# A four-layer convolution net on one core: start-up transfers on one queue, and M's first piece eight steps later

## The chip, the core and the metric

The kernel runs on one core of a Trainium2 chip. The core has five engines with instruction streams of their own: TensorE (matmul, PE in the profile), VectorE (DVE), ScalarE (ACT), GpSimd (POOL) and SyncE (SP, which here only issues transfers). A transfer is issued by an instruction of one of the engines and then moved by the core's DMA engines. The metric is the device time of one execution in microseconds (us), the median of several.

## The reference

The input is x, four images of 32 x 32 points with 16 channels. Four layers each add to x a function of its group norm. Three of them are position-dependent convolutions, the third in order is an interval layer:

```python
def conv(inputs, M, W, G):                    # layers 0, 1 and 3
    first = einsum('ijyx,byxc->bijc', M, inputs)
    shifted = conv_with_kernel(inputs, G)      # a 3x3x16x16 kernel for each of the 1024 points ij
    diff = relu(inputs[:, None, None] - shifted)
    second = einsum('ijyx,bijyxc->bijc', W, diff)
    return first - second

x = x + conv(gn(x), L0_M, L0_W, L0_G)
x = x + conv(gn(x), L1_M, L1_W, L1_G)
x = x + interval_layer(gn(x), W0, b0, W1, b1, W2, b2)
x = x + conv(gn(x), L3_M, L3_W, L3_G)
```

For each point ij, each of 16 output channels and each image, `shifted` is a whole 32 x 32 image, from a product over 9 x 16 = 144 inputs. That product is nearly all of the work. The term with M is one matrix product of 1024 x 1024 with the images.

## The kernel before

**Tiling.** The images are handled in two groups (g = 0, 1) of two images (b = 0, 1). A convolution layer of one group is a *phase*; with three convolution layers there are six. A phase runs over eight chunks t of 128 points each, and in a chunk over 16 channels f and two images b, so 32 *steps*. `conv_layer` writes out the steps. A step makes one 128 x 1024 product in a pair of PSUM banks: `first_part` (matmuls of `ib` and `ia` with the G's parts, then at L665 a scaling of the PSUM pair on ScalarE) and, one step later, `second_part` (matmuls of `iyz` and `im`, then at L682 on VectorE the minimum with zero, times W, summed). There are four PSUM pairs. In the steady state a step takes TensorE 1.57 us.

**Preparing G.** Four channels of a chunk are a *unit* u of 8 steps. `prep_parts` prepares each unit before it is used, a piece at each step: `raw` is loaded from HBM (L110), GpSimd subtracts a selection (L214, in `prep`), VectorE masks the upper bits (L203, `upper`), ScalarE makes W9 (L175, `halve`) and two of the parts (L236, L240), GpSimd the rest (L237, L238, L241, L243, L245). Last, two copies within SBUF, issued by SyncE, turn the halves of the partitions (L251, `parts<-parts`), and the `raw` of the unit after next is loaded. The first two units are taken as plain fp32 without this preparation, so the first 16 steps of the kernel run on other tiles (`raw`, `first`) and take 1.94 us each.

**Preparing the images.** For each image, `split` makes two parts (`ty` on ScalarE at L284, `tz` on VectorE or GpSimd at L280) in a tile `temp`. `place` then copies them to the partitions of `ia` (eight copies, L299) and `ib` (four copies, L302), and `difference` makes `iyz` (L288). In the first phase this is done by `rest_of_start` within the first steps, on VectorE, with `temp` a piece of the tile `first`; in later phases by `before_conv`, on GpSimd. `place` there is given a list of engines and issues its copies on them in turn: `[nc.sync, nc.scalar]` at the start (so ScalarE issues all copies of `tz`), `[nc.sync]` later.

**The term with M.** `load_first_terms` takes the tile `mt` and loads M in eight pieces of 512 KB, one every six steps (L416). `first_terms` then runs 128 matmuls (L427), two transposes (L434) and two additions to X (L437). `first`, `temp`, `mt` and the tables of the interval layer all have the same single buffer (`tag="big"`), so the first piece of M waits until the copies out of `temp` have read it.

**Order.** The schedule is the program's own: each engine runs its instructions in the order in which they are written. `behind(phase)` is a generator of the side work of a phase. `conv_layer` advances it after a step; the number that it yields is how many steps pass until it is advanced again, and the constants `IDLE` and `CALM` wait for a step at which the preparation of G leaves room. An instruction that waits holds up everything behind it on its engine, and this holds for an engine that issues a transfer too. The transfers of SyncE and ScalarE get one of eight semaphores in turn, in the order of the program, and each waits before its issue until the transfer that had the semaphore before has landed. An example: the eighth copy of an image, issued at 259.35 us, came directly after the landing at 259.33 us of the G that had been issued eight transfers earlier.

The constants `wv` and `bv` of the interval layer (L449, L450) and X of the second group (L739) are loaded by ScalarE.

Of the kernel before, what the change touches and what calls it, by code (L numbers as in the profile page):

```python
# [29 lines left out]
LAST = (H - 1) * HW  # L30
# [14 lines left out]
def net_kernel(ctx: ExitStack, tc: tile.TileContext, x, xq, xi, convs, iv_w, iv_b, out):  # L45
# [26 lines left out]
    nc = tc.nc  # L72
# [20 lines left out]
    X = [const.tile([P, NT, GC], F32, name=f"X{g}") for g in range(NG)]  # L93
# [80 lines left out]
    def halve(dst, src, mask):  # L174
        nc.scalar.activation(dst, src, AF.Copy, scale=mask[:, 1:2])  # L175
# [20 lines left out]
    def image(v, x):  # L196
        return v.rearrange("... (y x) -> ... y x", x=x)[..., :HW]
# [69 lines left out]
    def prep_plain_rest(u, at=0, to=FU):  # L267
        halve_rest(units[u][3][:, at:to], raws[u][:, 2, at:to], low_p)

    def halves(temp, b):  # L270
        v = temp.rearrange("p (k s b n) -> p k s b n", k=2, s=2, b=GB)
        return v[:, 0, :, b], v[:, 1, :, b]

    def split(eng, g, b, temp, name, pause=IDLE):

        ty, tz = halves(temp, b)
        high = upper(image(raw[:, :2, b], WP), 2, f"x{name}{b}")
        yield 1
        for s in range(2):
            eng.tensor_tensor(  # L280
                image(tz[:, s], HW), image(raw[:, s, b], WP), image(high[:, s], HW), ALU.subtract
            )
            yield pause
            nc.scalar.activation(ty[:, s], high[:, s], AF.Copy, scale=EPS)  # L284
# [2 lines left out]
        ty, tz = (v.bitcast(F32)[:, s] for v in halves(temp, b))  # L287
        eng.tensor_tensor(iyz[g][:, s, b], ty, tz, ALU.subtract)  # L288

    def place(engs, g, b, temp):  # L290

        ty, tz = (v.bitcast(F32) for v in halves(temp, b))
        da, db = (v[g].bitcast(F32)[:, :, b] for v in (ia, ib))
        k = 0
        for h, (lo, hi) in enumerate(QUARTERS):
            for s in range(2):
                at = HW if s == h else 0
                for to, src in ((lo, ty), (hi, tz)):
                    engs[k % len(engs)].dma_start(da[to, s, :LAST], src[lo, s, at : at + LAST])  # L299
                    k += 1  # L300
            for to, src in ((lo, ty), (hi, tz)):
                engs[k % len(engs)].dma_start(db[to], src[hi])  # L302
                k += 1
        yield 1


# [64 lines left out]
    def before_conv(g, layer):  # L371
        xn = work.tile([P, NT, GC], F32, tag="xn", bufs=2, name=f"xn_{g}_{layer}")
        xns[g] = xn
        yield from group_norm(g, f"c{g}{layer}", xn, 1 if layer == 2 else 4)

        nc.vector.transpose(
            xt[g][:, :, 1 : 1 + H], xn
        )  # L380
        inner = xs[g][:, :, WP : WP + H * WP].rearrange("p h (t r n) -> p h r t n", r=ROWS, n=WP)
        for r in range(ROWS):
            for h in range(2):
                nc.sync.dma_start(
                    inner[:, h, r], xt[g][GC * r : GC * (r + 1), :, HW * h : HW * h + WP]
                )
        yield 2
        xsv = xs[g].rearrange("(b c) h n -> c h b n", b=GB)
        for slot, row, tap in [
            (slot, row, tap) for slot in range(2) for row, tap in enumerate(TAPS[slot])  # L390
        ] + [(2, row, 8) for row in range(4)]:
            for h in range(2):
                off = tap // 3 * WP + tap % 3
                r0 = 64 * h + C * row
                nc.sync.dma_start(
                    raw[r0 : r0 + C, slot ^ h if slot < 2 else 2, :, :RUN], xsv[:, h, :, off : off + RUN]
                )
            if layer < 2 or row % 2:
                yield 1
        yield 6 if layer == 2 else 12  # L400
        temp = big.tile([P, 8192], F32R, tag="big", name=f"temp_{g}{layer}")[:, :TEMP]
        for b in range(GB):
            yield from split(nc.gpsimd, g, b, temp, f"{g}{layer}")
            yield IDLE
            halve(image(im9[g][:, b], HW), image(raw[:, 2, b], WP), low_x)
            yield from place([nc.sync], g, b, temp)
            for s in range(2):
                difference(nc.gpsimd, g, b, s, temp)
            yield 1
            halve_rest(image(im9[g][:, b], HW), image(raw[:, 2, b], WP), low_x)  # L410
            yield 1

    def load_first_terms(layer):
        mt = big.tile([P, NT, 4, 256], F32, tag="big", name=f"MT_{layer}")
        for pt in range(NT):
            nc.sync.dma_start(mt[:, pt], convs[layer][0][pt // (NT // 2)][:, pt % (NT // 2)])  # L416
            yield 6
        return mt
# [25 lines left out]
    wv = const.tile([P, 7, C], F32, name="wv")  # L444
    bv = const.tile([P, 3], F32, name="bv")
    iv = {}

    def constants():
        nc.scalar.dma_start(wv, iv_w)  # L449
        nc.scalar.dma_start(bv, iv_b)  # L450
        mask2 = const.tile([P, GB], F32, name="mask2")
        nc.vector.tensor_reduce(
            mask2, ident.rearrange("p (s b c) -> p b s c", b=GB, c=C), axis=AX.XY, op=ALU.add
        )

        nc.gpsimd.tensor_scalar_mul(mask2[GC : 2 * GC], mask2[GC : 2 * GC], -1.0)
        yield 2

        def blocks(dst, k, mask, n, p0=0):
            p = dst.shape[0]  # L460
            nc.gpsimd.tensor_tensor(
                dst,
                wv[p0 : p0 + p, k, :].unsqueeze(1).to_broadcast([p, n, C]),
                mask[p0 : p0 + p].unsqueeze(2).to_broadcast([p, n, C]),
                ALU.mult,
            )

        nc.gpsimd.memset(rt, 0.0)
        yield 1


        for k, hidden, name in ((0, None, "f0"), (3, 2, "f1"), (6, 5, "f2")):
            n = 64 if hidden is None else 96
            t = const.tile([n, GB, C], F32, name=name)
            blocks(t[:64], k, mask2, GB)
            if hidden is not None:
                blocks(t[64:], hidden, mask2, GB, 64)
            iv[name] = t.rearrange("p k c -> p (k c)")
            yield 1
        for k, name in ((1, "r0"), (4, "r1")):  # L480
            t = const.tile([64, NQ * GB, C], F32, name=name)
            for q in range(NQ):
                blocks(t[:, q * GB : (q + 1) * GB, :], k, mask2, GB)
            iv[name] = t.rearrange("p k c -> p (k c)")
            yield 1
# [249 lines left out]
    def behind(phase):  # L735
        g, layer = phases[phase]
        if phase == 0:
            yield from rest_of_start()
            nc.scalar.dma_start(X[1], x[1])  # L739
            zeros(1)  # L740
            yield 1
            yield from constants()
        if phase + 1 < len(phases):
            g1, layer1 = phases[phase + 1]
            if layer1 == 2:
                yield from interval_layer(g1)
            terms = g1 == NG - 1 and layer1 < NL - 1
            yield from before_conv(g1, layer1)
            if terms:
                mt = yield from load_first_terms(layer1)  # L750
                yield from first_terms(layer1, mt)
        if phase == len(phases) - 1:
            mt = yield from load_first_terms(layer)
            yield from first_terms(layer, mt)
            yield 4
            nc.sync.dma_start(out[1 - g], X[1 - g])
# [114 lines left out]
    def rest_of_start():  # L871

        nc.sync.dma_start(X[0], x[0])
        load_raw(2)
        load_raw(3)
        prep_plain_rest(0, F0, FU)
        for slot in (0, 1, 2):
            normal(nc.vector, 1, slot)
            sides(nc.vector, 1, slot)
        halve(image(im9[0][:, 1], HW), image(raw[:, 2, 1], WP), low_x)  # L880
        prep_plain(1)
        prep(2)
        yield 1
        halve_rest(image(im9[0][:, 1], HW), image(raw[:, 2, 1], WP), low_x)
        prep_plain_rest(1)
        yield 2
        temp = first.bitcast(F32R)[:, used : used + TEMP]
        for b in range(GB):
            yield from split(nc.vector, 0, b, temp, "00", 1)
            yield from place([nc.sync, nc.scalar], 0, b, temp)  # L890
            for s in range(2):
                difference(nc.vector, 0, b, s, temp)
            yield 1
        nc.gpsimd.memset(zero, 0.0)
        nc.vector.memset(part, 0.0)
        zeros(0)
        xns[0] = work.tile([P, NT, GC], F32, tag="xn", bufs=2, name="xn_00")
        yield from group_norm(0, "c00", xns[0], 4)
# [83 lines left out]
```

## Time and profile before

| | us |
|---|---|
| median of 3 runs | 2481.87 |
| lowest, highest | 2480.47, 2485.29 |
| the profiled execution | 2481.97 |
| its span, from the first to the last instruction | 2480.3 |

What each engine was busy with in five stretches of the span (the first numbers are start and end, then the length; x is the number of instructions; the last three are the granted clock of TensorE as a share, the mean share of busy DMA engines, and the GB/s that they moved):

```profile
core 0: us, PE busy (x) PEld busy (x) DVE busy (x) ACT busy (x) POOL busy (x), PEclk, DMA share, GB/s
0.00:46.00 46.00, 37.51 (x182) 18.79 (x182) 42.58 (x108) 11.72 (x20) 15.25 (x21) 1.00 0.73 215
46.00:56.00 10.00, 7.48 (x64) 5.94 (x66) 6.87 (x16) 6.89 (x9) 9.08 (x13) 1.00 0.32 74
56.00:248.00 192.00, 191.97 (x1716) 160.29 (x1714) 164.09 (x306) 150.62 (x178) 130.10 (x164) 1.00 0.57 156
248.00:276.00 28.00, 26.10 (x231) 21.21 (x229) 23.71 (x37) 19.87 (x23) 19.66 (x21) 1.00 0.76 196
276.00:447.00 171.00, 171.00 (x1593) 147.70 (x1591) 134.60 (x230) 126.03 (x144) 98.25 (x113) 1.00 0.55 153
```

The first phase runs from 0 to about 447 us. Between 56 and 248 us and from 276 us on, TensorE has no gap to speak of. The stretches 46 to 56 and 248 to 276 hold 2.5 and 1.9 us in which it ran no matmul.

How to read the lines below: a line of a timeline gives start, length, engine, line of the code, operation, what is written and read, and the count of equal instructions; in square brackets stands the idle time before, and what ended it. A "q" after the engine's name means its sequencer, the part that issues transfers. A chain or a wait names the instruction that came last before the waiting one could start. The landing of a transfer is when its last part had arrived.

### The profile page before, as it was taken

The numbers are of one execution on the slowest core, as the hardware profiler recorded it, in microseconds if no ns is written. First come the engines' busy times: TensorE is split into PE (matmuls) and PEld (weight loads), VectorE is DVE, ScalarE is ACT, GpSimd is POOL, SyncE is SP. The second block draws the span as 40 slices with busy tenths as digits, with TensorE's granted clock in tenths as the row PEclk, the third lists the DMA queues.
The fourth block names the chain that finished last, engine by engine and source line by source line (L and its number), as shares of the span: only waits on it lengthen the run. The fifth ranks groups of instructions, "written<-read, shape, count | busy, mean of one in ns | idle before, by whom it ended". The sixth has DMA issues, their size and how long they took to land.

```text
span 2480.3 us, 58060 instructions
## 1 busy us (share of the span) xinstructions
PE 2458.5 (99%) x21906; PEld 2074.2 (84%) x21906; DVE 2086.0 (84%) x3617; ACT 1878.2 (76%) x2181; POOL 1579.3 (64%) x1750
## 2 busy tenths in 40 slices
PE   8999999999999999999999999999999999999999
PEld 4888888888888888888888989888989888888887
DVE  8888878888888888788898988899889888788887
ACT  3778767787777778677777777787777787677776
POOL 4766655667555667555567777586778676555552
PEclk9999999999999999999999999999999999999999
DMA  6556744465454457544454545574455477554442
GB/s 189 140 144 183 213 131 134 138 180 157 137 145 137 137 157 193 176 137 137 137 145 119 143 126 139 146 195 124 129 139 145 120 187 201 150 145 137 137 137 54
DMA packets 97673, 366.92 MB, mean 148 GB/s; under 512 B 26480, under 2 KB 31472, under 8 KB 97392
## 3 DMA queue, kind: packets, MB, share of 16 engines
q1 hardware_dynamic: 95696, 361.57, 52.9%
q8 instruction: 172, 2.82, 0.5%
q10 hardware_dynamic: 1568, 1.62, 0.3%
q14 instruction: 109, 0.89, 0.1%
q0 software_dynamic: 128, 0.02, 0.0%
HBM read 199.78 MB, written 1.02 MB: 81 GB/s over the span
## 4 chain that ended last, share of the span: by engine, by line
PE 94%; DVE 2%; DMA 2%; issue 1%; ACT 1%; POOL 0%; SPq 0%; ACTq 0%; DVEq 0%; POOLq 0%
PE pc L629 92%; DVE junk L682 1%; PE pf L427 1%; DMA parts<-parts 1%; ACT pc L665 0%; DMA raw<-in_xi 0%; DMA raw<-in_g 0%; DMA ia<-first 0%; PE ps_l L550 0%; DMA first<-in_g 0%; PE ps_r L563 0%; DVE tables L510 0%; DVE raw L848 0%; DVE upper_w L203 0%; SPq L302 0%
## 5 line engine op out<-in xcount | busy, mean ns | idle before, releaser
L682 DVE SCALAR_TENSOR_TENSOR junk<-pc,WT 128x1024 f32<-128x1024 f32 x1536 | 1880.0, 1224 | 363.6 <-PE pc L629 316.8
L665 ACT ACTIVATE pc<-pc 128x1024 f32<-128x1024 f32 x1520 | 1531.8, 1008 | 556.1 <-PE pc L629 531.6
L629 PE MATMUL pc<-ib,parts 64*128 64x512 f32 x6080 | 953.0, 387 | 4.7 <-DVE junk L682 2.9
L629 PE MATMUL pc<-iyz,parts 64*128 64x512 f32 x6080 | 950.3, 387 | 5.3 <-ACT pc L665 5.2
L629 PE MATMUL pc<-ia,parts 64*128 64x496 f32 x6080 | 928.5, 379 | 0.0
L629 PEld LDWEIGHTS pc<-ib,parts 64*128 64x128 f32 x6080 | 585.1, 184 | 109.3 <-DVE junk L682 8.5
L629 PEld LDWEIGHTS pc<-ia,parts 64*128 64x128 f32 x6080 | 587.6, 184 | 106.2
L629 PEld LDWEIGHTS pc<-iyz,parts 64*128 64x128 f32 x6080 | 586.2, 184 | 94.9 <-ACT pc L665 9.4
L629 PE MATMUL pc<-im,W 64*128 64x496 f32 x3072 | 606.4, 384 | 0.0
L237 POOL TENSOR_TENSOR parts<-raw,upper_w 128x512 fp32r<-128x512 f32 x190 | 249.0, 1311 | 496.3 <-DVE upper_w L203 447.3
L629 PEld LDWEIGHTS pc<-im,W 64*128 64x128 f32 x3072 | 297.8, 184 | 57.3 <-issue 3.6
L243 POOL CAST parts<-parts 32x512 fp32r<-32x512 f32 x380 | 231.2, 608 | 48.8 <-ACT parts L240 30.5
L238 POOL TENSOR_TENSOR W<-W,raw 128x512 fp32r<-128x512 f32 x190 | 246.9, 1300 | 7.8 <-ACT W L175 7.8
L241 POOL TENSOR_TENSOR parts<-parts 128x512 fp32r<-128x512 f32 x190 | 246.5, 1297 | 2.2 <-ACT parts L236 2.0
L245 POOL CAST parts<-upper_w 32x512 fp32r<-32x512 f32 x380 | 231.6, 609 | 22.8
L214 POOL TENSOR_TENSOR raw<-raw,ident 128x512 f32<-128x512 f32 x190 | 199.5, 1050 | 61.5 <-DMA raw<-in_g 36.6
L175 ACT ACTIVATE W<-raw,low_w 128x512 fp32r<-128x512 f32 x190 | 136.2, 717 | 9.2 <-DMA ia<-first 9.2
L682 DVE DVE_READ_ACCUMULATOR junk<-pc,WT 128x1 f32 x1536 | 127.8, 83 | 0.0
L236 ACT ACTIVATE parts<-upper_w 128x512 fp32r<-128x512 f32 x190 | 118.8, 625 | 4.8 <-DVE upper_w L203 4.7
L240 ACT CAST parts<-upper_w 128x512 fp32r<-128x512 f32 x190 | 116.6, 614 | 0.0
L697 POOL TENSOR_SCALAR acc<-acc 128x32 f32<-128x32 f32 x40 | 16.7, 417 | 136.5 <-DVE junk L682 134.6
L203 DVE TENSOR_SCALAR upper_w<-raw 128x512 int32<-128x512 int32 x190 | 85.2, 449 | 2.7 <-POOL raw L214 2.3
(139 smaller groups left out, 479.1 us busy)
## 6 DMA issues: line engine op xcount, KB each, us to landing
raw<-in_g SPq DMA_DIRECT2D x190, 768.0 KB, 7.1
parts<-parts SPq DMA_DIRECT2D x380, 384.0 KB, 5.0
WT<-in_w SPq DMA_DIRECT2D x48, 512.0 KB, 4.6
MT<-in_mt SPq DMA_DIRECT2D x24, 512.0 KB, 7.9
raw<-xs SPq DMA_DIRECT2D x120, 71.8 KB, 3.1
ib<-temp SPq DMA_DIRECT2D x40, 128.0 KB, 2.4
ia<-temp SPq DMA_DIRECT2D x80, 62.0 KB, 3.4
raw<-in_xi SPq DMA_DIRECT2D x3, 287.0 KB, 5.0
```

The costliest lines, as they stand in the source:

```text
L175: nc.scalar.activation(dst, src, AF.Copy, scale=mask[:, 1:2])
L214: eng.tensor_tensor(raws[u][:, s, at:to], raws[u][:, s, at:to], pick[s][:, f0 + at : f0 + to].unsqueeze(2).to_broadcast([P, to - at, P]), ...
L236: nc.scalar.activation(WD, high, AF.Copy, scale=-EPS)
L237: nc.gpsimd.tensor_tensor(WL, w8, high, ALU.subtract)
L238: nc.gpsimd.tensor_tensor(W9, W9.bitcast(F32), src[:, 2], ALU.add)
L240: nc.scalar.copy(WU, high)
L241: nc.gpsimd.tensor_tensor(WD, WD.bitcast(F32), WL.bitcast(F32), ALU.add)
L243: nc.gpsimd.tensor_copy(WU[hi], WL[lo].bitcast(F32))
L245: nc.gpsimd.tensor_copy(WL[lo], high[hi])
L629: nc.tensor.matmul(ps[:, h, at : at + n], lhsT=w[r], rhs=v[r] if n == NH else v[r][:, :n], start=first and k == 0, stop=k == len(pairs) - ...
L665: nc.scalar.activation(ps, ps, AF.Copy, scale=1.0 + EPS)
L682: nc.vector.scalar_tensor_tensor(junk, ps.rearrange("p h n -> p (h n)"), 0.0, chunks[n], op0=ALU.min, op1=ALU.mult, accum_out=accs[phase][ ...
```

## The change

The list of engines goes from `place`: all its copies, those of the first two images too, are issued by SyncE. X of the second group, `wv` and `bv` are loaded by SyncE as well. ScalarE keeps only the three transfers at the very beginning (L139, L141). In `load_first_terms` a `yield 8` stands between taking the tile and the first load, so that M's pieces, and all that follows in the side work, come eight steps later in each of the three layers.

```diff
-    def place(engs, g, b, temp):
+    def place(g, b, temp):
 
         ty, tz = (v.bitcast(F32) for v in halves(temp, b))
         da, db = (v[g].bitcast(F32)[:, :, b] for v in (ia, ib))
-        k = 0
         for h, (lo, hi) in enumerate(QUARTERS):
             for s in range(2):
                 at = HW if s == h else 0
                 for to, src in ((lo, ty), (hi, tz)):
-                    engs[k % len(engs)].dma_start(da[to, s, :LAST], src[lo, s, at : at + LAST])
-                    k += 1
+                    nc.sync.dma_start(da[to, s, :LAST], src[lo, s, at : at + LAST])
             for to, src in ((lo, ty), (hi, tz)):
-                engs[k % len(engs)].dma_start(db[to], src[hi])
-                k += 1
+                nc.sync.dma_start(db[to], src[hi])
         yield 1
...
-            yield from place([nc.sync], g, b, temp)
+            yield from place(g, b, temp)
...
         mt = big.tile([P, NT, 4, 256], F32, tag="big", name=f"MT_{layer}")
+        yield 8
         for pt in range(NT):
...
-        nc.scalar.dma_start(wv, iv_w)
-        nc.scalar.dma_start(bv, iv_b)
+        nc.sync.dma_start(wv, iv_w)
+        nc.sync.dma_start(bv, iv_b)
...
-            nc.scalar.dma_start(X[1], x[1])
+            nc.sync.dma_start(X[1], x[1])
...
-            yield from place([nc.sync, nc.scalar], 0, b, temp)
+            yield from place(0, b, temp)
```

In the order of the instructions this gives the following. On SyncE, at the start, the copies of an image stand as twelve in a row ahead of unit 2's L251 and L110 (image 0) and behind them (image 1). X, `wv` and `bv` stand between unit 6's L110 and unit 7's L251. In the first two layers, M's first piece stands behind one more pair of L251 and L110 than before. On TensorE and VectorE the matmuls with M, the two transposes and the two additions come eight steps later; the rest of their order, and all of GpSimd's, is as before.

## The prediction

> **What bounds the kernel now.** I read the page first (busy shares, then the chain that ended last), then the stretches of TensorE's timeline in which it has gaps, then what ScalarE and SyncE did in front of those gaps.
>
> ```profile
> PE 2458.5 (99%) x21906; PEld 2074.2 (84%) x21906; DVE 2086.0 (84%) x3617; ACT 1878.2 (76%) x2181; POOL 1579.3 (64%) x1750
> PE 94%; DVE 2%; DMA 2%; issue 1%; ACT 1%; POOL 0%; SPq 0%; ACTq 0%; DVEq 0%; POOLq 0%
> ```
>
> TensorE is busy for 99% of the span and is 94% of the chain. So only a gap of TensorE, or work added to it, can move the time. Summed over the span, gaps over 0.05 us between its matmuls come to 13.4 us. Two of them stand in the first 10 us, where the statistics of the input are awaited; of the others all but three are under 0.8 us. Those three lie near what the diff touches. Two are at the start, here each with the row ahead of it (TensorE's timeline):
>
> ```profile
> 44.73 0.62 PE L629 MATMUL pc<-ia,parts 64*128 64x496 f32 x4
> 46.90 0.73 PE L629 MATMUL pc<-iyz,parts 64*128 64x512 f32 x4 [1.55 <-ACT pc L665]
> ...
> 52.87 0.60 PE L629 MATMUL pc<-ia,parts 64*128 64x496 f32 x4
> 55.10 0.74 PE L629 MATMUL pc<-iyz,parts 64*128 64x512 f32 x4 [1.63 <-ACT pc L665]
> ```
>
> Both end with ScalarE's scaling of the PSUM pair (L665). ScalarE's timeline says why it was late:
>
> ```profile
> 35.59 5.89 ACTq L299 DMA_DIRECT2D ia<-first x2
> 41.52 0.64 ACTq L302 DMA_DIRECT2D ib<-first x1
> 42.20 1.25 ACTq L299 DMA_DIRECT2D ia<-first x2
> 43.49 0.64 ACTq L302 DMA_DIRECT2D ib<-first x1
> 44.18 0.72 ACT L175 ACTIVATE W<-raw,low_w 128x512 fp32r<-128x512 f32 x1 [9.18 <-DMA ia<-first]
> ...
> 53.50 0.63 ACT L236 ACTIVATE parts<-upper_w 128x512 fp32r<-128x512 f32 x1 [1.48 <-DVE upper_w L203]
> 54.04 1.01 ACT L665 ACTIVATE pc<-pc 128x1024 f32<-128x1024 f32 x1
> ```
>
> From 35.0 to 44.18 ScalarE computes nothing. It issues its six copies for image 1, and its second one holds the semaphore that unit 4's G (issued 31.76) had before; that transfer landed at 40.90, and the copy went out at 40.97. Behind it wait L175 of unit 3 and then the first L665, hence the 1.55 us. GpSimd's L238 waits for that L175, so its whole preparation of unit 3 and the L214 of unit 4 are late too; L214 ends at 53.0, VectorE's L203 of unit 4 waits for it, ScalarE's L236 for that, and the second L665 is queued behind L236: the 1.63 us. The chain of waits runs through the same steps.
>
> The third gap is at 273.6 (TensorE's timeline, then SyncE's):
>
> ```profile
> 275.34 0.49 PE L629 MATMUL pc<-ib,parts 64*128 64x512 f32 x1 [1.71 <-DMA parts<-parts]
> ```
> ```profile
> 261.19 1.61 SPq L302 DMA_DIRECT2D ib<-temp x2
> 264.73 0.33 SPq L416 DMA_DIRECT2D MT<-in_mt x1
> 265.18 1.15 SPq L251 DMA_DIRECT2D parts<-parts x2
> ```
>
> M's first piece takes the buffer that `temp` had, so SyncE holds it until the last copy out of `temp` has landed (264.65). Unit 20's copies (L251) stand behind it, though GpSimd had finished their source at 260.8. They then land behind M's 512 KB: the second one at 275.30, 9.55 us after its issue, where one with a free queue takes 5.1 us.
>
> **What the Trainium skill says.** "DMA: Bandwidth & Descriptors", section "Issuing engines are not separate DMA queues": transfers of all engines run on the same 16 DMA engines, and issuing from several saves only sequencer time. The trace agrees: ScalarE's copy issued at 35.59 landed at 41.56, between two of SyncE's (41.34, 41.80). The same page, section "Anatomy of one DMA": a wait for a semaphore happens on the issuing sequencer before dispatch. That is ScalarE at 35.59 and SyncE at 262.8 to 264.73. "SBUF — State Buffer" states in its rules that a VectorE operation with two SBUF inputs and a GpSimd operation that reads SBUF block each other. The trace fits: the two L288 on VectorE took 2.13 us at 29.93, beside GpSimd, and 1.29 us at 40.04, with GpSimd idle.
>
> **The change part by part.**
>
> *Image 0's twelve copies on SyncE alone.* One copy costs SyncE 0.54 to 0.66 us. Later images already do this; from the fourth copy to the end of the twelfth it took 6.3 us (from 946.77) and 6.5 us (from 233.49). In the changed order the fourth waits for VectorE's second L280, which ends at 27.5, so the twelfth ends near 33.9. Unit 2's copies (L251), at 30.06 now, then issue at 33.9 and land near 39.5 (36.57 now). TensorE takes them at 43.3: hidden with 3.8 us to spare, and the images' parts land before that.
>
> *Image 1's twelve.* They stand behind unit 2's copies and unit 4's G. The same sequence, with nothing else late, is at 248.92 and at 962.20: from the first L251 to the last landing 15.7 us (264.65) and 14.0 us (976.18). From 33.9 that gives 47.9 to 49.6, against 45.89 now. TensorE needs these parts at its fifth step of unit 2, near 49.35 in the changed kernel (below). So the cover here is 1.4 us at best, and 0.25 us is lost at worst.
>
> *What goes from ScalarE.* L175 of unit 3 starts at 35.0 instead of 44.18; L236 waits for L203 (ends 37.65). GpSimd ends its L237 at 39.0 and goes on with L238 at once instead of at 44.98: its chain moves 6.0 us earlier, so L214 of unit 4 ends at 47.0 instead of 53.0, and unit 3's copies issue at 45.9 instead of 51.91.
>
> *What is late next.* The first L665 starts 1.1 us after its first matmul (43.31) and takes 1.0, so TensorE goes on at 45.5 where it would be ready at 45.1: of the 1.55 us, 0.35 stays. Then TensorE's steps, 1.57 us each, put the fifth step's first matmul at 49.35 and the second half of that step at 51.9 if nothing waits. VectorE: last junk of the plain steps until 46.8, then L682, L326 and L329 (0.95 us), L682, so L203 of unit 4 runs near 50.3 to 50.7 without a wait; L236 (0.63) until 51.3, L665 until 52.2, TensorE at 52.25. Now this point is at 55.10: **2.85 us gained** at the start. Bounds: all of the two gaps, counted between starts of neighbouring matmuls (1.94 and 2.00 us, each less the normal 0.22), is 3.5; if L288 and L203 are slowed by GpSimd's earlier work (0.8 us by the difference of the two L288 above) and image 1's parts come at 49.6, it is 1.8.
>
> *X[1], wv, bv on SyncE.* They stand between unit 6's G (95.6) and unit 7's copies (110.27), where SyncE waits for 13 us; three issues are 1.15 us. ScalarE's issues at 105.6 to 108.0 stood beside its own work and ended no gap. Cost nothing, either way; if SyncE had no such pause, it would be the 1.15 us.
>
> *M eight steps later.* Eight steps are one unit, so in all three layers the matmuls with M and the transposes after them keep their place within a unit and keep their 7.04 us. In layer 0 SyncE issues unit 20's copies at 262.85 and its next G at 264.0, then M. The copies land at about 262.85 + 0.5 + 5.1 = 268.4, or a bit later behind image parts in flight, and are used at 273.0. The interval at 273.25 is 2.10 us and goes to 0.22: **1.88 us gained**. Next is unit 21: its copies now land at 286.23, 1.5 us before use, and then have one piece of M ahead of them instead of two. In layer 1 (from 976.40) the same order left no gap; the copies landed 0.5 us before use, so nothing is won. In the last layer no gap stands near M. M's last piece now comes behind a WT (issued 328.5, landed 333.0), so lands near 336, and is used at 330.3 + 12.5 = 342.8.
>
> Sum: 2.85 + 1.88 = 4.7. The profiled execution took 2481.97 us (span 2480.3, and 1.7 around it), so 2477.2 us. It lies 0.1 above the median of the runs shown, 2481.87.
>
> **Rivals.**
> - *The gaps close wholly* (2.85 becomes 3.5): 2481.97 - 5.4 = 2476.6. For it: VectorE and ScalarE have slack at the fifth step of a few tenths. Against it: the first L665 can't start before its matmuls.
> - *Only M's part pays*: image 1's parts, or VectorE beside a GpSimd that is 6 us earlier, put a wait where the old ones were. With about 0.3 us gained at the start: 2481.97 - 2.2 = 2479.8. For it: image 1's last landing is about at the moment of use.
> - *Slower*: image 1's last five copies can't issue before unit 4's G has landed, since eight transfers at most are in flight. If that G is late, each us beyond 49.35 + 0.4 is a us of TensorE. With M's gain counted, the time is the old one when the last copy lands at 54.5 and 0.2% worse from 59.5 on; at 62 it is 2489.5. For it: a copy issued behind a G took 8.2 us (251.36), and G itself 9.2. Against it: G would have to land 10 us later than the two sequences above say.
>
> **How the numbers follow.** A measurement of this kernel tells about 0.2% (5.0 us) from no change; below 2476.9 counts as faster. The forecast of 2477.2 has a chance of 0.66, own range 2475.5 to 2479.0, and so falls on both sides of that line (0.31 faster, 0.35 same). Wholly closed: 0.16, faster. Only M: 0.08, same. Slower: 0.10. Together 0.47, 0.43, 0.10. The range from 2474.6 to 2481.0 takes in the first three with the scatter of medians (2480.5 to 2485.3 among single runs) and leaves the slower case out.
>
> **What would show it.** Right, if ScalarE runs L175 of unit 3 near 35, GpSimd's L214 of unit 4 ends near 47, TensorE has two gaps of at most 0.5 us between 43 and 53 and none at 273, and M's first piece stands behind L251 and L110 on SyncE. Wrong, if TensorE waits near 49 for a copy into ia or ib, or for unit 2 at 43.3, or if a new wait for L251 stands at 286, 986 or in the last layer.

## The result, and the profile after

| | before | after |
|---|---|---|
| median, us | 2481.88 | 2478.24 |
| lowest, highest, us | 2478.3, 2487.26 | 2475.26, 2480.68 |
| span of the profiled execution, us | 2480.3 | 2476.7 |

The ratio of after to before is 0.9982, with a 95% interval of 0.9976 to 0.9988: 4.5 us less, between 3.0 and 6.0. The forecast was 2477.2 us, with a range of 2474.6 to 2481.0. Line numbers differ a little from kernel to kernel: the matmul L629 of before is L627 in after, the scaling L665 is L663, and the copies L299 and L302 are L298 and L300. "Before" and "after" below are the two kernels, and their profiles where a time is given; "the changed kernel" is after.

The page of after, its busy shares and the shares of the chain that ended last:

```profile
PE 2458.2 (99%) x21906; PEld 2090.1 (84%) x21906; DVE 2087.3 (84%) x3617; ACT 1878.4 (76%) x2181; POOL 1579.7 (64%) x1750
PE 94%; DVE 2%; issue 1%; DMA 1%; ACT 0%; SPq 0%; POOL 0%; ACTq 0%; DVEq 0%; POOLq 0%
```

TensorE's busy time differs by 0.3 us from before. So the span fell by gaps that closed, and the table by stages of after says where (columns as in the table of before):

```profile
46.00:56.00 10.00, 9.38 (x83) 8.27 (x81) 8.77 (x23) 7.32 (x9) 5.99 (x6) 1.00 0.76 200
56.00:248.00 192.00, 191.97 (x1716) 187.91 (x1714) 164.19 (x302) 150.71 (x178) 129.39 (x162) 1.00 0.56 152
248.00:276.00 28.00, 27.52 (x246) 22.70 (x244) 24.74 (x40) 21.42 (x25) 20.55 (x23) 1.00 0.86 220
```

From 46 to 56 us TensorE runs 9.38 us instead of 7.48, from 248 to 276 us 27.52 instead of 26.10; in between nothing changed. The same matmul compared in both traces tells it more exactly. The second half of the fifth step of unit 2, the second of the two stall points of before, starts at 52.91 instead of 55.10: 2.19 us earlier. The first half step behind M's gap starts at 275.90 before, and at 272.04 in after: 3.87 earlier (before rounding), so 1.68 more. The end is 3.60 earlier.

The starts of ScalarE's and GpSimd's work for the units 3 and 4, in after (timelines of the two engines):

```profile
34.93 0.71 ACT L175 ACTIVATE W<-raw,low_w 128x512 fp32r<-128x512 f32 x1
```
```profile
38.98 1.28 POOL L238 TENSOR_TENSOR W<-W,raw 128x512 fp32r<-128x512 f32 x1
...
45.94 1.04 POOL L214 TENSOR_TENSOR raw<-raw,ident 128x512 f32<-128x512 f32 x1
```

L175 of unit 3 starts 9.25 us earlier, and L214 of unit 4 ends 6.0 us earlier. Of the two waits for L665 0.09 us of the first is left, and nothing of the second. What is late next is a wait of another kind (TensorE's timeline, then the chain of waits in front of it):

```profile
49.51 0.39 PE L627 MATMUL pc<-ib,parts 64*128 64x512 f32 x1
50.52 0.69 PE L627 MATMUL pc<-ib,parts 64*128 64x512 f32 x3 [0.62 <-DMA ib<-first]
...
52.91 0.81 PE L627 MATMUL pc<-iyz,parts 64*128 64x512 f32 x4
```
```profile
35.39 10.06 DMA raw<-in_g
45.45 0.02 issue
45.47 0.53 SPq L298
...
47.98 2.39 DMA ib<-first
50.38 0.14 issue
50.52 9.56 PE pc L627 x82
```

Unit 4's G is in flight for 10.06 us, from 35.39 to 45.45. SyncE gets to image 1's copies at 36.69, issues the first seven of them, and then holds the next one until that G has landed. The remaining ones go out from 45.47 on, and the last lands at 50.38, when TensorE has already begun the fifth step. The hold moved from ScalarE, where compute stood behind it, to SyncE, where only transfers do.

At M, SyncE's timeline in after:

```profile
260.92 1.15 SPq L251 DMA_DIRECT2D parts<-parts  x2
262.17 1.16 SPq L110 DMA_DIRECT2D raw<-in_g  x1
263.51 1.48 SPq L414 DMA_DIRECT2D MT<-in_mt  x1
```

Unit 20's copies are ahead of M's first piece, and the second one lands 5.1 us after its issue, at 266.56, instead of 9.55 after. TensorE has no gap between 270 and 276.

### The profile page after: what moved, and what is told of

It reads as the page before. It is cut to its first block, busy times and chain, and to the rows that moved or that the text cites. A ratio compares the mean times of both kernels' runs of the same rounds, so it can differ in the third digit from the quotient of the medians.

```text
span 2476.7 us, 58058 instructions
## 1 busy us (share of the span) xinstructions
PE 2458.2 (99%) x21906; PEld 2090.1 (84%) x21906; DVE 2087.3 (84%) x3617; ACT 1878.4 (76%) x2181; POOL 1579.7 (64%) x1750
## 4 chain that ended last, share of the span: by engine, by line
PE 94%; DVE 2%; issue 1%; DMA 1%; ACT 0%; SPq 0%; POOL 0%; ACTq 0%; DVEq 0%; POOLq 0%
PE pc L627 93%; DVE junk L680 1%; PE pf L425 1%; DMA raw<-in_g 1%; ACT pc L663 0%; DMA first<-in_g 0%; SPq L298 0%; DVE raw L846 0%; SPq L300 0%; PE ps_l L548 0%; PE ps_r L561 0%; DMA parts<-parts 0%; DVE tables L508 0%; DVE raw L854 0%; DMA ib<-first 0%
## 5 line engine op out<-in xcount | busy, mean ns | idle before, releaser
L663 ACT ACTIVATE pc<-pc 128x1024 f32<-128x1024 f32 x1520 | 1532.0, 1008 | 561.0 <-PE pc L627 535.8
L627 PE MATMUL pc<-ib,parts 64*128 64x512 f32 x6080 | 958.5, 388 | 4.1 <-DVE junk L680 3.4
L627 PE MATMUL pc<-iyz,parts 64*128 64x512 f32 x6080 | 955.5, 387 | 2.2 <-ACT pc L663 2.0
L627 PE MATMUL pc<-ia,parts 64*128 64x496 f32 x6080 | 933.5, 379 | 0.0
L627 PEld LDWEIGHTS pc<-ia,parts 64*128 64x128 f32 x6080 | 595.5, 184 | 100.8
L627 PEld LDWEIGHTS pc<-ib,parts 64*128 64x128 f32 x6080 | 591.5, 184 | 105.0 <-DVE junk L680 9.9
L627 PEld LDWEIGHTS pc<-iyz,parts 64*128 64x128 f32 x6080 | 592.5, 184 | 88.4 <-ACT pc L663 6.4
L627 PE MATMUL pc<-im,W 64*128 64x496 f32 x3072 | 611.5, 384 | 0.0
L627 PEld LDWEIGHTS pc<-im,W 64*128 64x128 f32 x3072 | 303.0, 184 | 54.5 <-issue 3.2
L238 POOL TENSOR_TENSOR W<-W,raw 128x512 fp32r<-128x512 f32 x190 | 247.6, 1303 | 1.8 <-ACT W L175 1.8
L214 POOL TENSOR_TENSOR raw<-raw,ident 128x512 f32<-128x512 f32 x190 | 199.9, 1052 | 52.2 <-DMA raw<-in_g 28.7
L175 ACT ACTIVATE W<-raw,low_w 128x512 fp32r<-128x512 f32 x190 | 136.2, 717 | 0.1
L203 DVE TENSOR_SCALAR upper_w<-raw 128x512 int32<-128x512 int32 x190 | 86.1, 453 | 1.2 <-POOL raw L214 0.9
```

What stands on the lines that cost most here:

```text
L214: eng.tensor_tensor(raws[u][:, s, at:to], raws[u][:, s, at:to], pick[s][:, f0 + at : f0 + to].unsqueeze(2).to_broadcast([P, to - at, P]), ...
L238: nc.gpsimd.tensor_tensor(W9, W9.bitcast(F32), src[:, 2], ALU.add)
L627: nc.tensor.matmul(ps[:, h, at : at + n], lhsT=w[r], rhs=v[r] if n == NH else v[r][:, :n], start=first and k == 0, stop=k == len(pairs) - ...
L663: nc.scalar.activation(ps, ps, AF.Copy, scale=1.0 + EPS)
```

## The experiments

In what follows "the lead" is how much earlier the second half of the fifth step starts than before, where it is at 55.10. It measures the part at the start, free of what comes later. In after it is 2.19.

It is not free of what comes earlier, though. Unit 2's first matmul stands ahead of both gaps, and it doesn't start at the same moment in every profile: at 43.31 in before, at 43.33 in after, and anywhere from 42.66 to 43.92 in the others. The changed kernel itself, in a second profile, has it 0.6 us earlier than before (before, then that second profile, TensorE):

```profile
43.31 0.63 PE L629 MATMUL pc<-ib,parts 64*128 64x512 f32 x4
...
42.69 0.63 PE L627 MATMUL pc<-ib,parts 64*128 64x512 f32 x4
```

So where profiles are compared a second number is given, "the net lead", which is counted from that matmul. In after it is 2.21. Two kernels whose start is that of before (M alone and the constants alone, below) have a net lead of 0.48 and 0.55 all the same, because their first gap was 1.04 and 1.06 us and not 1.55. A difference of half a us between two single profiles is thus seen without any change at the start.

**The images' parts alone, and M alone.** The first is the kernel before with

```diff
-            yield from place([nc.sync, nc.scalar], 0, b, temp)
+            yield from place([nc.sync], 0, b, temp)
```

> The kernel before, with the first images' copies on SyncE alone; X, wv and bv stay on ScalarE and M's pieces keep their place. My theory (ScalarE held by its own copies of image 1): L175 of unit 3 at 35, the two gaps of 1.55 and 1.63 us go and one of about 0.6 us near 50 takes their place, TensorE is 2.2 us ahead from 53 us on, the gap of 1.7 us at 273 stays (at about 271.4). Time 2.2 us below before, ratio 0.9991. Rival (the start's gain is only borrowed and is lost again before 273): TensorE is ahead by 2.2 us at 53 and by under 0.7 us at 250.

The second is the kernel before with only `+        yield 8` ahead of M's pieces.

> The kernel before, with M's pieces eight steps later and nothing else. My theory: both gaps at the start stay (1.55 and 1.63 us), the gap at 273.6 goes, unit 20's second copy lands at 268 to 269 instead of 275.3; time 1.9 us below before, ratio 0.9992. Rival (M's later pieces collide with unit 21 or 22 instead): a gap of 1 us or more appears between 280 and 320, and the time is within 1 us of before.

Against the runs of before beside them (median 2483.75) they took 2479.48 and 2480.0: ratios 0.9984 (0.9978 to 0.9991) and 0.9985 (0.9978 to 0.9991). Each part pays in this set. The images' part had a lead of 2.08 (net 2.38), L175 of unit 3 at 35.22, and a wait of 0.48 us for ib at 50.4, as in after. The lead was not lost again on the way: M's gap began at 270.87, where before had it at 273.63. That gap was kept, in two parts (TensorE's timeline):

```profile
272.15 0.49 PE L629 MATMUL pc<-ib,parts 64*128 64x512 f32 x1 [1.28 <-DMA parts<-parts]
273.83 0.79 PE L629 MATMUL pc<-ib,parts 64*128 64x512 f32 x1 [1.19 <-DMA parts<-parts]
```

M alone had no gap there, and kept the two at the start (TensorE's timeline):

```profile
46.38 0.73 PE L630 MATMUL pc<-iyz,parts 64*128 64x512 f32 x4 [1.04 <-ACT pc L666]
...
54.59 0.73 PE L630 MATMUL pc<-iyz,parts 64*128 64x512 f32 x4 [1.62 <-ACT pc L666]
```

So the two gains are separate, each with its own gap. Their timed gains add up to 7.7 us (0.31%), though, against 4.5 for the whole. Each is known to about 1.6 us only, so the timed runs can't size the shares; the part "Sum" below comes back to it.

**Image 1 alone.** Image 0's copies stay on both queues, image 1's go on SyncE:

```diff
-            yield from place([nc.sync, nc.scalar], 0, b, temp)
+            yield from place([nc.sync, nc.scalar] if b == 0 else [nc.sync], 0, b, temp)
```

> The kernel before, with image 1's copies on SyncE alone, image 0's on both queues as before, M as before. My theory (only image 1's copies hold ScalarE; and SyncE is free for image 1 about 4 us sooner): L175 of unit 3 at 35, no wait for ScalarE at 45 or 53, image 1's last landing at 46 to 48, no gap over 0.3 us near 50; TensorE 2.6 to 3.0 us ahead at 55, time 2.8 us below before. Rival (image 0's copies on ScalarE matter as well): the gaps of 1.55 and 1.63 us stay in good part, gain under 1.5 us.

2479.54, ratio 0.9983 (0.9977 to 0.999). The lead was 2.39, under the expected 2.6, because unit 2 began late, at 43.87; the net lead was 2.96. L175 ran at 34.88. Image 1's last copy landed at 46.34, four us earlier than in after, and TensorE waited for no copy. Of the gaps at the start one is left (TensorE's timeline):

```profile
46.07 0.73 PE L629 MATMUL pc<-iyz,parts 64*128 64x512 f32 x4 [0.24 <-ACT pc L665]
```

The gain at the start thus comes from image 1's six copies on ScalarE. Moving image 0's brings nothing beyond it, and makes image 1's parts later. Six profiles have image 0's copies on SyncE too and G in its old place (after, the images' parts alone, and four of those below); in each TensorE waited for ib, 0.39 to 0.96 us, and the net lead was 1.91 to 2.46. The timed ratios (0.9983 here, 0.9984 for both images) don't tell the two orders apart.

This profile shows one thing more. M's first piece stands ahead of unit 20's copies here, as in before, and the second of these landed 9.18 us after its issue, at 271.64. Yet there is no gap: TensorE needed the copy just then, and the row of four matmuls was only stretched, 1.06 us instead of 0.62 (TensorE's timeline):

```profile
271.12 1.06 PE L629 MATMUL pc<-ib,parts 64*128 64x512 f32 x4
```

So the gap at M is not there in every execution.

**Unit 4's G ahead of image 0's copies,** in the changed kernel, which takes it out of the row that image 1's copies wait in:

```diff
-            load_raw(u + RAWS)
+            if u > PLAIN:
+                load_raw(u + RAWS)
...
+            if b == 0:
+                load_raw(4)
             yield from place(0, b, temp)
```

> The changed kernel, with unit 4's G loaded ahead of image 0's copies instead of ahead of image 1's. My theory (what is left of the gain was lost because image 1's last five copies wait for the landing of unit 4's G): G issues near 25.5 and lands near 32, image 1's last copy lands near 47 instead of 50.4, the gap of 0.62 us at 50.2 goes, and TensorE is 0.6 to 0.8 us ahead of the changed kernel from 55 us on; time 0.7 us below it. Rival (image 0's copies and unit 2's L251 then come too late): a wait for a copy stands at 43.3, and it is slower than the changed kernel.

2478.6, ratio 0.9975 (0.9967 to 0.9983). G was issued at 24.87 and landed at 30.56, image 1's last copy landed at 46.62, and the wait at 50 was gone. The lead was 3.11 (net 2.76). In place of the wait (TensorE's timeline):

```profile
51.99 0.73 PE L628 MATMUL pc<-iyz,parts 64*128 64x512 f32 x4 [0.27 <-ACT pc L664]
```

By the net leads the changed kernel is 0.55 us behind this one here, and 0.63 us in the second pair of profiles below. Neither difference is beyond the scatter named above, but they go with the wait: with it the net lead was 2.46 at most in six profiles, and without it 2.76 at least in three (image 1 alone, and this kernel twice). So image 1's late landing cost the changed kernel about 0.6 us.

**Unit 4's G loaded twice,** to price the slower rival: in the changed kernel a second, equal load stands behind the first, ahead of image 1's copies.

```diff
+            if u == PLAIN:
+                nc.sync.dma_start(raws[4], convs[0][2][4 // NU, 4 % NU])
```

> The changed kernel, with unit 4's G loaded twice, the second time after the first has landed, both ahead of image 1's copies. It computes the same. It doubles the transfer that image 1's copies stand behind. My theory (the price of the slower case of the forecast: each us that image 1's parts are later is a us of TensorE): the first G lands near 43, the second is issued then and lands near 49, image 1's twelve copies issue from 44 on and the last lands near 54; the gap at 49.5 becomes 4 to 5 us and the time is 3.5 to 4.5 us above the changed kernel. Rival (TensorE's slack later in the first phase absorbs it): gap at 50, but under 1 us of difference at the end.

2482.74, ratio 1.0000 (0.9992 to 1.0008): by the ratios 4.5 us above the changed kernel, and the whole gain was gone. Image 1's last copy landed at 52.54, 2.16 us later than in after, and TensorE waited 2.49 us for it. The second half of the fifth step came 3.73 us later than in after, 1.57 more than the copy. The table by stretches of this kernel (matmuls in the first pair of brackets; the third number from the end is TensorE's granted clock) says why:

```profile
53.00:54.00 1.00, 1.00 (x6) 0.92 (x6) 0.00 (x0) 0.00 (x0) 1.00 (x1) 0.50 1.01 190
54.00:55.00 1.00, 1.00 (x8) 0.92 (x6) 0.00 (x0) 0.28 (x1) 0.12 (x1) 0.50 0.96 277
...
57.00:58.00 1.00, 1.00 (x13) 0.96 (x11) 0.46 (x3) 0.92 (x1) 0.89 (x2) 1.00 0.93 375
```

TensorE is busy throughout, but starts 6 to 8 matmuls per us instead of 13. After the gap the clock was at half for 3.413 us, which costs up to 1.7 us more.

**The constants alone.** The kernel before with X of the second group, `wv` and `bv` on SyncE:

```diff
-        nc.scalar.dma_start(wv, iv_w)
+        nc.sync.dma_start(wv, iv_w)
...
-            nc.scalar.dma_start(X[1], x[1])
+            nc.sync.dma_start(X[1], x[1])
```

> The kernel before, with only X of the second group, wv and bv loaded by SyncE. My theory: no effect; TensorE's gaps at 45.3, 53.5 and 273.6 stay as they were, no new one near 105, time within 1 us of before. Rival (ScalarE's issues there delayed a scaling): ScalarE's L665 near 105 to 108 comes earlier and a gain of 0.5 us or more shows at 110.

2484.58, ratio 1.0001 (0.9993 to 1.0009): nothing. SyncE issues them between 96.85 and 100.3, in its pause, and ScalarE's scalings near 105 keep their distance of 1.57 us.

**How far M must be moved.** The changed kernel with `yield 2` instead of `yield 8`, and the changed kernel with the delay in the later layers only (`if layer:` ahead of the `yield 8`), which undoes M's part in the first layer:

> The changed kernel, but M's pieces two steps late instead of eight: M's first piece stands ahead of unit 20's L251 as in the kernel before, and only the second and third piece come later. My theory (the hold of the queue for temp, and the first piece's bytes ahead of L251, made the gap): SyncE still goes on only when the last copy out of temp has landed, unit 20's second copy lands at 271 to 274 on a time scale where it is needed at 269.4, the gap at that point is 1.5 to 2.5 us, time 1.9 us above the changed kernel. Rival (the bytes of the second and third piece made it): no gap over 0.4 us there, time equal to the changed kernel.

> The changed kernel, with the eight steps in the last two layers with M only, the first layer as in the kernel before. My theory: the gain lies in the first layer alone, so the gap of 1.5 to 2.1 us near 270 is back and the time is 1.9 us above the changed kernel (2.2 below before). Rival (the shift also gains or costs in the later layers): more than 0.7 us of difference from that, seen as gaps between 960 and 1000 or in the last layer.

They took 2481.36, ratio 0.9994 (0.9986 to 1.0002), and 2481.42, ratio 0.9996 (0.9989 to 1.0002), where before took 2482.41. By the times neither is told from before. Both have the gap back, smaller than expected: 0.80 us with `yield 2`, where the rival had none, and in the second (TensorE's timeline):

```profile
272.00 0.50 PE L628 MATMUL pc<-ib,parts 64*128 64x512 f32 x1 [0.85 <-DMA parts<-parts]
```

With `yield 2` M's first piece is issued at 262.58, still ahead of unit 20's copies, and the second of these lands at 272.46. In the second kernel they land 7.4 and 9.6 us after their issues. The traces of after and of the second kernel don't differ near M in the later layers. So M's gain is in the first layer alone, and it takes a delay that puts M behind L251.

**Which of two things M does to unit 20's copies.** M's first piece could hold SyncE, or its 512 KB could stand ahead of the copies. In the second kernel of the last pair, M's first piece is cut so that a quarter of it (128 KB) is issued where the whole was, and the other three behind unit 20's copies (`src` is the piece of M):

```diff
...
+            if layer == 0 and pt == 0:
+                nc.sync.dma_start(mt[:, 0, :1], src[:, :1])
+                yield 6
+                continue
+            if layer == 0 and pt == 1:
+                nc.sync.dma_start(mt[:, 0, 1:], convs[0][0][0][:, 0, 1:])
...
```

> The kernel e6 (M not delayed in the first layer), with only a quarter (128 KB) of M's first piece ahead of unit 20's L251; the other three quarters go with the second piece. My theory (SyncE's hold for temp costs little by itself, the 512 KB ahead of L251 make the gap): SyncE is held as in e6, but unit 20's second copy lands 1.5 to 3 us sooner after its issue than e6's 9.6 us, and the gap of 0.85 us near 271.5 goes; unit 21's copies then land at most 1 us late or just in time. Rival (the hold is the cause): the gap near 271 stays at 0.8 us or more.

2479.64, ratio 0.9981 (0.9974 to 0.9989). The quarter landed 2.2 us after its issue, unit 20's second copy 5.85 us after its own, and no gap was there. The missing gap alone would prove little, since image 1 alone had none either. The landing tells more: with the whole piece ahead the second copy took 8.9 to 9.7 us in all seven profiles. The first load into M's buffer still waits for the same copies and stands at the same place in the queue; it is the bytes ahead that made the gap.

**Where the hold at the start belongs.** On one chip: the changed kernel again, the one with unit 4's G first again, and the kernel before with G first, in which both queues are kept:

> The changed kernel itself, beside the three others of this set on the same chip. 4 to 5 us below before; a gap of 0.5 to 1 us near 50, none near 270.

> The kernel e4_g_first, now beside the changed kernel. No gap near 50 but one of 0.3 us at 52, TensorE 0.7 to 1.0 us ahead of the changed kernel at 55; time 0.9 us below the changed kernel, which is less than its runs scatter, so the two intervals will overlap.

> The kernel before, with unit 4's G loaded ahead of image 0's copies; both images' copies stay on SyncE and ScalarE in turn, M as before. My theory (ScalarE was held because the semaphore of its copy was that of a slow transfer, not because it issues copies): ScalarE issues its six copies of image 1 from 35.6 to 41 or earlier without the hold of 5 us, L175 of unit 3 starts near 41 instead of 44.18, GpSimd's L214 of unit 4 ends near 50, the gaps at 45 and 53 shrink to 0.4 and at most 0.5 us, TensorE is 2.4 us or more ahead at 55. Time 2.5 us below before. Rival (issuing six copies is itself too long for ScalarE): L175 of unit 3 still after 43, and 1 us or more of the gaps stays.

| kernel | median, us | ratio, 95% interval | lead, us | net lead, us |
|---|---|---|---|---|
| before | 2483.72 | | | |
| changed | 2478.88 | 0.9980, 0.9973 to 0.9988 | 2.97 | 2.35 |
| changed, G first | 2477.75 | 0.9978, 0.9968 to 0.9988 | 3.18 | 2.98 |
| before, G first | 2481.38 | 0.9995, 0.9987 to 1.0004 | 1.44 | 1.92 |

In this profile the changed kernel waited 0.51 us for ib at 49.3. Its lead of 2.97 looks better than the 2.19 of after, but only because unit 2 began at 42.69; the net leads of the two differ by 0.14. G first took that wait away again (0.22 us for the scaling is left), but its intervals overlap those of the changed kernel in both comparisons. That it is faster is not shown by the times.

The third kernel met neither theory in full. G was out of image 1's way, yet the lead was only 1.44 and the net lead 1.92, where 2.4 or more was expected. ScalarE's timeline:

```profile
26.32 5.71 ACTq L300 DMA_DIRECT2D ia<-first  x2
...
40.48 1.51 ACTq L300 DMA_DIRECT2D ia<-first  x2
...
42.72 0.72 ACT L175 ACTIVATE W<-raw,low_w 128x512 fp32r<-128x512 f32 x1 [4.45 <-DMA ib<-first]
```

The hold went over to image 0's copies: ScalarE's second one waits there from 26.91 to 31.49. ScalarE's work on image 1's `first` (L284 of before) came late by it, at 37.12 instead of 33.85. Then ScalarE issued image 1's six copies from 37.56 to 42.67 without a hold, and L175 started at 42.72. So two things in the old order delay L175: a copy that waits for an earlier transfer, and the issuing itself, 5.1 us for six copies with the work between them. Only taking the copies off ScalarE removes both.

## Why the prediction was right

The time lay in the range, and both mechanisms, ScalarE's held copies and the bytes ahead of unit 20's copies, are the ones that the runs show. Still, one of the signs that the prediction gave of being wrong did appear: TensorE waited near 49 for a copy into ib, for 0.62 us in after and 0.51 us in the second profile, which is also more than the 0.5 us that it allowed. And part of the agreement in the time is luck, as the sum below shows.

*Image 0's copies on SyncE alone.* Said: the twelfth ends at 33.9, unit 2's copies issue then and land at 39.5. Measured: 34.06, 34.16 and 39.81; no wait at 43.3.

*What goes from ScalarE.* Said: L175 at 35.0, L238 at once, L214 of unit 4 until 47.0, L203 of unit 4 at 50.3 to 50.7. Measured: 34.93, 38.98, 46.98, 50.31. These came from durations in the old trace alone. The image-1 run shows that this is the cause of the gain, and the run with G first on two queues that the six issues count without a hold too. The lower bound took L288 and L203 as slowed by GpSimd. Measured, image 1's two L288 took 1.35 us and L203 of unit 4 took 0.42, against 1.29 and 0.43 before: nothing that shows. L203 reads one input only, so the rule that the prediction quotes doesn't speak of it.

*What is late next, at the start.* Said: of the first gap 0.35 us stays. In after the start of that half step is 0.71 behind the row ahead of it, where 0.45 is usual: 0.26. Right.

*Image 1's twelve: the mis-sized term.* Said: the last lands at 47.9 to 49.6, with a cover of 1.4 us at best and 0.25 us lost at worst. Measured: 50.38, and the interval at 49.51 is 1.01 us, 0.8 more than usual. In the two later sequences that I took it from, G took 9.2 and 6.6 us to land; this one took 10.06 us. The start therefore gave a net lead of 2.21 in after and 2.35 in the second profile of the same kernel, where the forecast was 2.85 with bounds of 1.8 and 3.5. Where image 1's copies were in time it gave 2.76 and 2.98 (G first) and 2.96 (image 1 alone), so the rest of the sum at the start had the right size.

*Unit 3's copies.* Said: issued at 45.9. Measured: 48.71, since SyncE was still at image 1's. I had counted when their source was ready and forgotten the queue that I had just filled. They landed at 55.62, and TensorE has no wait for them, so it cost nothing.

*X[1], wv, bv:* nothing said, nothing measured.

*M eight steps later.* Said: 1.88 us, layer 0 alone, unit 20's copies landing at 268.4. Measured: 1.68 between the two points in the traces, with a gap near 253 that is 0.3 us longer in after counted against it; 266.56; nothing in the later layers. The mechanism that was named, bytes ahead in the DMA engines, is the one that the run with a quarter of M shows. The size is one draw, however. With M's first piece ahead the gap was 1.71, 2.47 (in two parts), 0.80, 0.85, 0.85 and 1.74 us in six profiles, and in a seventh (image 1 alone) there was none. In two of them (the images' parts alone, and before with G first) a further 3.413 us at half clock followed, up to 1.7 us of work. The forecast knew neither the scatter nor that.

*Sum.* 4.7 forecast; 3.6 between the profiled spans, 4.5 (3.0 to 6.0) timed. The gaps gave about one us less than forecast. The time comes nearer, and that is luck: a term that the forecast didn't have, TensorE's clock, stands in for the shortfall. The record has the mean granted clock of each run, to three digits, and one stretch of 3.413 us at half takes 0.0007 off. Of the 155 runs of before beside the experiments 89 have 0.999 or 0.998; of the 36 runs of the changed kernel, 2. In the three sets of before the runs at 1.000 average 2481.5 to 2482.7 us, and all runs 1.1 to 1.5 us more. So 1.1 to 1.5 us of the timed gain, by this estimate, went with stretches at half clock that the changed kernel rarely has. (The end of an execution, after the last matmul, is at half clock as well, for 0.2 to 2.6 us in the profiles; from 2.5 us on this alone gives 0.999, as in the second profile of the changed kernel with G first. So not each 0.999 is such a stretch.)

The drops go with M's gap more than with those at the start. The six experiments that leave M's first piece whole and ahead of L251 have 40 of 102 runs below 1.000; M alone, which keeps both gaps at the start, has 2 of 21. That fits with M alone being timed at 3.7 us (2.2 to 5.5), where its gap in before was 1.7; how much of it the clock makes up is not shown.

It stays open why the images' part was timed at 4.0. The second kernel of the pair on M's delay is the same but for the constants and M in the later layers, where nothing was found, and it was timed at 1.0 (0.5 more to 2.7 less), on another chip. So one set of runs sizes a part less well than its interval says, and 7.7 against 4.5 shows no interplay of the two parts. Gaps elsewhere come and go too: near 1634 us, the changed kernel has 0.53 us in one profile and none over 0.2 in the other.

*The slower rival.* Its mechanism is real: one more G ahead of image 1 takes the whole gain. Its price was too low, though. It said one us of TensorE for each us of lateness; 2.16 us of lateness cost 3.73, the clock included.

## What to carry to other kernels

A transfer belongs on a queue with nothing urgent behind it: ask of each issuing engine what computes next, and what its copies wait for, since the wait and the issues both delay that work. A large load that nobody needs soon goes behind small copies that somebody does, in the order of issue; half a megabyte ahead of them cost nothing in one profile here and 0.8 to 2.5 us in six others, before what the clock adds. When a row of transfers is put on one queue, write down when everything behind it issues, and take the landing of the large loads in it with their scatter, not with the mean of two good cases. And count a gain in a profile from a mark just ahead of the change, not from the start of the execution.

## What was not expected of the hardware

The clock fell after short gaps. The Trainium skill ("TensorE: Matmul & The Clock Gate", Part 1) says that TensorE goes to half clock after an idle window of about 3.4 us, counted by a free-running window of 3413 ns. The runs agree on the half, and on the window: between two changes of the clock lies a whole number of such windows (11 in the kernel with G twice; 76 in the images' parts alone and in before with G first). They don't agree on how much idling it takes, as no gap named here was that long.

The traces show what it takes here. Count the windows from the moment at which the clock first rises, and add up TensorE's idle time in each. In the 14 profiles the full clock fell after each of the 17 windows with 51% or more idle, and after none of the others, of which the highest has 48%. Fourteen of the 17 are at the end, where the matmuls stop. The three others had 74% (the gap of 2.49 us), 66% (parts of the gaps of 1.28 and 1.19 us) and 51% (the gap of 1.74 us). Two pairs of windows, the first in before with G first, the second in before; columns as in the tables by stages, the granted clock third from the end:

```profile
270.90:274.31 3.41, 1.67 (x15) 1.08 (x13) 1.83 (x4) 1.01 (x1) 0.00 (x0) 1.00 1.00 350
274.31:277.73 3.42, 3.42 (x20) 2.75 (x18) 1.12 (x1) 1.01 (x1) 1.04 (x1) 0.50 1.07 269
...
52.37:55.79 3.42, 1.79 (x16) 1.18 (x16) 2.61 (x4) 2.29 (x4) 2.88 (x3) 1.00 0.82 189
55.79:59.20 3.41, 3.41 (x34) 2.81 (x32) 3.15 (x10) 2.30 (x3) 3.23 (x5) 1.00 0.82 265
```

With 1.74 us idle in one window the clock fell; with 1.63 us it did not. The gap of 1.71 us at M in before is no counterexample: a boundary of the windows, at 274.24, cuts it into 0.6 and 1.1 us. Since the windows lie differently in each execution, one and the same gap can have a drop behind it in some executions and none in others. Where one came it cost up to 1.7 us of work on top of the gap (1.57 us later than the copy explains, with G twice).

The time of one and the same 768 KB load of G varied from 5.7 us (G first, ahead of image 0's copies) to 10.06 (in after, ahead of image 1's). Where eight later issues hang on its landing, that scatter goes into the span.
